# Masked maxima of the latent scores: a mask added and minimised by VectorE in place of mask products on TensorE, for query blocks 3, 2 and 0

## The chip, the cores and the metric

The kernel runs on one core of a Trainium2 chip. The metric is the device time of one execution in microseconds (us), the median of the runs that were taken. A core has five engines that work side by side, each through its own queue in order: TensorE (PE in the profile, with its weight loads as PEld), VectorE (DVE), ScalarE (ACT), GpSimd (POOL) and SyncE (SP, which here issues DMAs). Operands lie in SBUF, 128 partitions wide; TensorE writes its products to PSUM, which has eight banks of 128 x 512 f32.

## What is computed

The input is 8 sequences of 512 tokens with 128 channels. Three blocks follow each other:

```
x = x + 0.5 * ffn(layernorm(x))     # two layers of local attention and a gated feed-forward
x = x + attn(layernorm(x))          # "latent" attention, causal, 16 heads of 8 channels
x = x + 0.5 * ffn(layernorm(x))     # the same two layers again
```

The change lies in the middle block, whose core is

```
q_lat = einsum('bqhd,hdl->bhql', q, k_eff)
attn  = einsum('bhql,bkl->bhqk', q_lat, c_kv) / sqrt(hs)
attn  = softmax(where(causal, attn, -inf))
y_lat = einsum('bhqk,bkl->bhql', attn, c_kv)
```

The kernel folds the weight matrices beforehand, so that a head is a product of 8 channels of a projected q with 8 channels of a projected k.

## The kernel before

The program has three parts, in this order: the first feed-forward part `ffn("f0")`, `latent_attention()`, and the second feed-forward part `ffn("f1")`. The two `ffn` parts are written out by a planner (`Plan`) with step costs and due times; the diff leaves it alone. The latent part is written in program order, and TensorE keeps that order (`in_order`). The other engines follow from the data.

**Layout of the latent part.** Each of the 16 heads lies in a quarter of the partitions (`quadrant(g)`, 32 partitions, g from 0 to 3) and a place j from 0 to 3. A product of two 32-partition slices uses one quarter of the rows of TensorE's array, so products of different g can run beside each other. The queries of a sequence are cut into NB = 4 blocks of P = 128.

**Two passes over the scores.** The softmax needs a maximum per query before it takes exponentials. So the scores of a sequence are formed twice. The *maxima* pass forms them with queries on the partitions (tile `sc`), masks them causally and takes the maximum along the keys. The negative maxima are collected in the tile `lnm` (`maxima_of(b)[0]`), transposed by TensorE (tile `tp_nm`, L1524), copied to SBUF (L1530) and sent by a DMA (L1534) into a spare row of q. The *sums* pass forms the scores again with keys on the partitions (tile `st`), with the maximum already subtracted through that row. ScalarE takes their exponentials from PSUM (L1565, tile `pl`), and TensorE multiplies those with the values (L1571, tile `lo`).

**Ten pieces, four quadrants.** `SUMS` and `MAXIMA` each cut the work of one sequence into ten pieces that fill a PSUM bank of 512 columns. For the maxima they are: four pieces of query block 3 alone (512 keys), four of block 2 (384 keys) beside block 0 (128 keys), and two of block 1 for two heads (2 x 256 keys):

```
MAXIMA = (
    [[((3, j), 0)] for j in range(4)]
    + [[((2, j), 0), ((0, j), 3 * P)] for j in range(4)]
    + [[((1, j), 0), ((1, j + 1), 2 * P)] for j in (0, 2)]
)
```

The loop in `latent_attention` runs over the sequences b = 0 to 6. For each it goes through the ten pieces of the sums of sequence b and takes with each one piece of the maxima of sequence b + 1; each piece is done for the four quadrants. This text calls one quadrant of one such pair of pieces a *unit*: 7 x 10 x 4 = 280 units in the latent part. Sequence 0's maxima are done by the plan of `f0`, the sums of sequence 7 by the plan of `f1`.

**One unit.** `by_turns` deals the TensorE instructions of `sum_products` (bank `st`) and `maximum_products` (bank `sc`) alternately. Each list opens with four mask products in bf16 (L1545, L1487), which write the causal mask into the diagonal blocks of the bank, and then adds the products of q and k in f32 (L1554, L1496), one for each query block held. Each f32 product shows up as two records in the trace. Then ScalarE takes the exponentials of `st`, and `maximum` reduces `sc` on VectorE with one TENSOR_REDUCE of 512 columns: L1513 writes straight to `lnm`, L1509 (blocks 2 and 0) writes partial maxima of 128 columns to `lnb`. `maxima_end` (L1520, L1521) merges `lnb` into `lnm` once per sequence.

**PSUM.** The latent part has eight banks in one ring, `unit_bank`. A unit takes two, so TensorE can be at most four units ahead of the slower of ScalarE and VectorE.

**Between the units.** After five of the ten pieces, and again after the tenth, TensorE does other work of the sequence: transposes of earlier results (L1654), which VectorE divides by the sums (L1579, L1580) and GpSimd adds to X (L1586), products with the values (L1571), and projections of a later sequence (L1622, L1627, L1635). So each sequence has two stretches of 20 units, called stretch 1 (the four pieces of block 3 and the first of blocks 2 and 0) and stretch 2 (the other three of blocks 2 and 0 and the two of block 1), with TensorE's other work in the gaps between them. After stretch 2, TensorE transposes the maxima (L1524) before it goes on.

One operation elsewhere matters as a model: in the local attention of `ffn`, L777 is `nc.vector.tensor_tensor_reduce` on 128 x 128 scores in PSUM with a mask tile in SBUF; it adds, scales and keeps the minimum in an accumulator output.

Of the kernel before, what the change touches and what calls it, by code (L numbers as in the profile page):

```python
# [9 lines left out]
F32 = mybir.dt.float32  # L10
BF16 = mybir.dt.bfloat16
AF = mybir.ActivationFunctionType
ALU = mybir.AluOpType
# [3 lines left out]
P = 128  # L17
MASKED = -1.0e30
# [253 lines left out]
def kernel(  # L272
# [21 lines left out]
    nc = tc.nc  # L294
    B, T, C = x.shape
# [99 lines left out]
    def quadrant(g):  # L395
        return slice(32 * g, 32 * g + 32)
# [1199 lines left out]
    def latent_attention():  # L1596
        def in_order(ins):
            tc.keep_in_program_order(ins)

        count = [0]  # L1600

        def unit_bank(name):
            count[0] += 1
            return psum["s"].tile([P, 512], F32, tag="sc", name=f"{name}_{count[0]}")

        dealt = [0]

        def two_tiles():
            tag, *first, shape = PLACES[dealt[0] % len(PLACES)]
            dealt[0] += 1  # L1610
            if first:
                return [
                    flat(wk.tile(shape, F32, tag=f"{tag}{first[0] + n}", name=f"pl{dealt[0]}_{n}"))
                    for n in range(2)
                ]
            t = flat(wk.tile(shape, F32, tag=tag, name=f"pl{dealt[0]}"))
            return [t[:, :512], t[:, 512:]]

        def turn_into(xT, xn, b):
            tp = unit_bank(f"tp_lat_{b}")  # L1620
            for i in range(NB):
                in_order(nc.tensor.transpose(tp[:, i * P : (i + 1) * P], xn[:, i], ident))  # L1622
            nc.scalar.copy(xT, tp)

        def project(n, b, xT):
            ps = unit_bank(f"pq_{b}")
            in_order(nc.tensor.matmul(ps, lhsT=full[n], rhs=xT, start=True, stop=True))  # L1627
            fl = wk.tile([P, T], F32, tag=f"ge{n}", name=f"fl{n}_{b}")
            nc.scalar.copy(fl, ps)
            spread(heads("qk"[n], b), fl, "qk"[n])  # L1630

        def project_values(b, xT):
            ps = unit_bank(f"pv_{b}")
            for i in range(NB):
                in_order(nc.tensor.matmul(  # L1635
                    ps[:, i * C : (i + 1) * C], lhsT=xT[:, i * P : (i + 1) * P], rhs=full[2],
                    start=True, stop=True,
                ))
            value_copy(heads("v", b), ps)

        def multiply(b, j, todo):

            o = unit_bank(f"lo_{b}")
            for n, (c, at, tiles) in enumerate(todo):
                for ins in value_part(b, j, c, at, tiles, o, n == 0, n == NB - 1):
                    in_order(ins)
            os_ = wk.tile([P, INNER // P, P], F32, tag=f"oT{j % 2}", name=f"os_{b}_{j}")
            nc.scalar.copy(flat(os_), o)
            updates.append((b, j, flat(os_)))

        def update(b, j, os_):
            tp = unit_bank(f"tp_o_{b}")
            for i in range(NB):
                in_order(nc.tensor.transpose(  # L1654
                    tp[:, i * P : (i + 1) * P], os_[:, i * P : (i + 1) * P], ident
                ))
            rs = wk.tile([P, NB, 4], F32, tag=f"lrs{j % 2}", name=f"lrs_{b}_{j}")
            on = wk.tile([P, NB, 4, MD], F32, tag=f"lon{j % 2}", name=f"lon_{b}_{j}")
            quotients(tp, rs, on)
            add_tokens(b, j, on)  # L1660

        updates = left["updates"]
        ready = left["values"]
        turned, normed = {}, {}

        def norm(b):
            normed[b] = wk.tile([P, NB, C], F32, tag=f"hs{b % 2}", name=f"xn_{b}")
            ln_apply(normed[b], X[:, b], f"lat_{b}")

        norm(2)  # L1670
        ahead = [(b, held) for b in range(1, B) for held in MAXIMA]

        def heads_ahead(b):
            xT = turned[b] = wk.tile([P, T], F32, tag=f"fT{b % 2}", name=f"xT_{b}")
            turn_into(xT, normed.pop(b), b)
            return lambda: [project(n, b, xT) for n in range(2)]

        heads_ahead(2)()
        for b in range(B - 1):
            parts = {}  # L1680
            for s, held in enumerate(SUMS):
                other = ahead.pop(0) if ahead else None
                tiles = {}
                for half in (0, 1):
                    two = two_tiles()
                    for n in range(2):
                        g = 2 * half + n
                        bank = unit_bank(f"st_{b}")
                        units = [sum_products(b, held, g, lambda bank=bank: bank)]
                        if other is not None:  # L1690
                            mb, mheld = other
                            mbank = unit_bank(f"sc_{mb}")
                            units.append(
                                maximum_products(mb, mheld, (g + 2) % 4, lambda mbank=mbank: mbank)
                            )
                        by_turns([
                            [lambda ins=ins: in_order(ins()) for ins in unit] for unit in units
                        ])
                        sum_exponential(two[n], bank)
                        tiles[g] = two[n]  # L1700
                        if other is not None:
                            maximum(maxima_of(mb), mheld, (g + 2) % 4, mbank)
                for (c, j), at in held:
                    parts.setdefault(j, []).append((c, at, tiles))
                    if len(parts[j]) == NB:
                        ready.append((b, j, parts[j]))


                if s == len(SUMS) // 2 - 1:
                    while updates:  # L1710
                        update(*updates.pop(0))
                    project_ahead = heads_ahead(b + 2) if 0 < b < B - 2 else None
                    while ready:
                        multiply(*ready.pop(0))
                    if project_ahead is not None:
                        project_ahead()
            while updates:
                update(*updates.pop(0))
            if b > 0:
                project_values(b + 1, turned.pop(b + 1))  # L1720
            m = maxima_of(b + 1)
            maxima_end(m)
            tp = unit_bank(f"tp_nm_{b + 1}")
            in_order(maxima_turn(m, tp))
            shift_in(b + 1, shift_rows(b + 1, tp))
            while ready:
                multiply(*ready.pop(0))
            if b + 3 < B:
                norm(b + 3)
# [92 lines left out]
```

## Time and profile before

| what | value |
|---|---|
| median of 3 runs | 1708.36 us (1701.99 to 1709.99) |
| the profiled execution, whole | 1703.49 us |
| its span, first to last instruction | 1701.7 us |
| mean granted TensorE clock | 0.991 of full speed |
| busy over the span | PE 96%, DVE 79%, ACT 78%, POOL 68% |
| units of the latent part, first to last reduction | 726.7 to 989.4 us |
| VectorE reductions of the units: L1513 / L1509 | 168 / 112, mean 0.68 us each |
| mask products of the maxima (L1487) | 1120 in the units, four in each |

The span is the time from the first to the last instruction. The page gives busy shares over the whole span, and the stages of this kernel differ: GpSimd is nearly idle in the latent part and busy in the others. A duration is the time from the start to the end of one instruction; two instructions in a row on VectorE overlap a little, so the distance from start to start is shorter than the duration. The view by windows gives each engine's busy time in a stretch of the span, the timeline gives instructions in order of time with their start, and the view of waits gives who waited for whom.

### The profile page before, as it was taken

The page shows a single profiled execution, that of the slowest core. Times are in us where ns is not written, and L with a number is a line of the kernel's source. Part 1 is how long each engine was busy: PE and PEld are TensorE (multiplying, and loading weights), DVE is VectorE, ACT ScalarE, POOL GpSimd, SP SyncE. Part 2 cuts the span into 40 slices and gives each one's busy share as a digit, 9 for nine tenths or more (in the row PEclk, how much of TensorE's full clock was granted, in tenths as well). Part 3 has the DMA queues.
Part 4 walks back from the last instruction along what each step waited for, and adds up shares of the span by engine and source line. Part 5 has one row for each costly group of instructions (what it writes and reads, how often), then busy time and mean ns, then how long its engine had stood idle before and what let it go on. Part 6 is the DMA issues. An engine that isn't in the chain of part 4 may idle for free. (4 is left out here: it accounts for less than half of the span.)

```text
span 1701.7 us, 51528 instructions
## 1 busy us (share of the span) xinstructions
PE 1633.8 (96%) x19360; PEld 1146.6 (67%) x19360; DVE 1339.2 (79%) x4484; ACT 1329.3 (78%) x3913; POOL 1161.6 (68%) x1919
## 2 busy tenths in 40 slices
PE   5999999999999999999999999999999999999997
PEld 2666666676776676577777755766766666676675
DVE  6988888888888885867776655988888888888884
ACT  4888888888888885267766667988888888888883
POOL 8999998888788887000000056999887888878882
PEclk9999999999999999999999999999999999999998
DMA  5110111111111110000000001111111111111111
GB/s 168 29 36 20 27 26 27 33 27 28 35 27 26 27 30 9 16 17 17 17 16 17 16 9 29 33 27 26 27 26 27 27 32 30 28 31 26 27 30 41
DMA packets 51560, 49.48 MB, mean 29 GB/s; under 512 B 22726, under 2 KB 34544, under 8 KB 51312
## 3 DMA queue, kind: packets, MB, share of 16 engines
q1 hardware_dynamic: 51168, 45.41, 11.1%
q8 instruction: 153, 2.51, 0.6%
q14 instruction: 95, 0.78, 0.2%
q10 hardware_dynamic: 144, 0.79, 0.1%
HBM read 6.30 MB, written 2.10 MB: 5 GB/s over the span
## 5 line engine op out<-in xcount | busy, mean ns | idle before, releaser
L785 ACT ACTIVATE pr_f<-pr_f,nm_f 128x128 f32<-128x128 f32 x1024 | 397.4, 396 | 0.8 <-DVE nm_f L777 0.7
L634 PE MATMUL mm_f<-wqkv,hT_f 128*128 128x512 f32 x768 | 388.8, 600 | 1.7 <-DVE hT_f L612 1.4
L668 POOL TENSOR_TENSOR qk_f<-c_f,s_f 128x512 f32<-128x512 f32 x256 | 325.8, 1275 | 64.6 <-DVE s_f L647 30.7
L777 DVE CUSTOM_DVE_ANT_0 pr_f<-sc_f,band,q_f 128x128 f32<-128x128 f32 x1024 | 293.5, 345 | 46.9 <-PE sc_f L769 46.6
L792 POOL TENSOR_TENSOR pr_f<-pr_f,rso_f 128x512 f32<-128x512 f32 x256 | 264.9, 1042 | 12.6 <-DVE rso_f L811 7.9
L644 DVE TENSOR_TENSOR c_f<-mm_f,tab 128x512 f32<-128x512 f32 x256 | 174.2, 680 | 50.2 <-PE mm_f L634 31.5
L1586 POOL TENSOR_TENSOR X<-X,lon 128x128 f32<-128x128 f32 x26 | 11.3, 457 | 280.4 <-DVE lon L1580 280.4
L785 ACT ACTIVATION_READ_ACCUMULATOR pr_f<-pr_f,nm_f 128x1 f32 x1024 | 198.9, 194 | 0.0
L596 PEld LDWEIGHTS mm_f<-ident,qk_f 128*128 128x128 f32 x1024 | 121.3, 141 | 93.6 <-issue 63.4
L943 PE MATMUL mm_f<-fT_f,w 128*128 128x512 f32 (+1 forms) x384 | 182.2, 603 | 0.0
L647 DVE TENSOR_TENSOR s_f<-mm_f,tab 128x512 f32<-128x512 f32 x256 | 174.1, 680 | 0.0
L1565 ACT ACTIVATE pl<-st 128x512 f32<-128x512 f32 x280 | 156.0, 596 | 19.0 <-PE sc L1496 5.9
L660 ACT ACTIVATE sq_f<-mm_f 128x512 f32<-128x512 f32 x256 | 149.9, 595 | 21.5 <-PE mm_f L634 16.0
L852 PEld LDWEIGHTS mm_f<-pT_f,V_f 128*64 128x64 f32 x4096 | 130.2, 138 | 53.9 <-issue 23.9
L697 DVE TENSOR_REDUCE squares<-sq_f 128x16 f32<-128x1024 f32 x128 | 155.2, 1213 | 14.0 <-ACT sq_f L660 14.0
L596 PE MATMUL mm_f<-ident,qk_f 128*128 128x128 f32 x1024 | 156.3, 276 | 4.5 <-POOL qk_f L711 3.5
L596 PEld LDWEIGHTS mm_f<-ident,pr_f 128*128 128x128 f32 x1024 | 118.6, 141 | 55.9 <-POOL pr_f L792 26.5
L596 PE MATMUL mm_f<-ident,pr_f 128*128 128x128 f32 x1024 | 148.2, 275 | 6.5 <-POOL pr_f L792 6.0
L876 PEld LDWEIGHTS mm_f<-wo,oT_f 128*128 128x128 f32 x1024 | 129.7, 192 | 35.0 <-issue 18.9
L852 PE MATMUL mm_f<-pT_f,V_f 128*64 128x64 f32 x4096 | 147.7, 225 | 0.2 <-ACT pT_f L833 0.2
L634 PEld LDWEIGHTS mm_f<-wqkv,hT_f 128*128 128x128 f32 x768 | 122.0, 193 | 37.0 <-issue 24.3
L769 PE MATMUL sc_f<-kT_f,qT_f 64*64 64x128 f32 x4096 | 141.6, 276 | 0.0
(184 smaller groups left out, 3875.5 us busy)
## 6 DMA issues: line engine op xcount, KB each, us to landing
V_f<-V_f SPq DMA_DIRECT2D x224, 128.0 KB
hs_f<-Y SPq DMA_DIRECT2D x32, 112.0 KB
X<-in_x_dram SPq DMA_DIRECT2D x8, 256.0 KB
out_dram<-hs_f SPq DMA_DIRECT2D x6, 256.0 KB
Y<-fl SPq DMA_DIRECT2D x32, 32.0 KB
kT_f<-fl SPq DMA_DIRECT2D x32, 32.0 KB
V_f<-fl SPq DMA_DIRECT2D x32, 32.0 KB
wqkv<-in_wqkv_dram ACTq DMA_DIRECT2D x1, 768.0 KB
```

The costliest lines, as they stand in the source:

```text
L596: nc.tensor.transpose(dst[:, i * P : (i + 1) * P], src(i), ident)
L634: nc.tensor.matmul(ps.tile, lhsT=hT[:, i * P : (i + 1) * P], rhs=wqkv_sb[l][:, at * INNER : (at + 1) * INNER], start=True, stop=True,)
L644: nc.vector.tensor_mul(c1.tile, psv, tabs[l][:, 2 * s, i].unsqueeze(1).to_broadcast([P, H, DH]))
L647: nc.vector.tensor_mul(s1.tile.rearrange("p h (t d) -> p h t d", t=2), psv.rearrange("p h (t d) -> p h t d", t=2)[:, :, ::-1], tabs[l][:, ...
L668: lambda s=s, c1=c1, s1=s1: nc.gpsimd.tensor_add(qk[:, s].rearrange("p (h d) -> p h d", d=DH), c1.tile, s1.tile),
L697: nc.vector.tensor_reduce(z[:, 0], sq.tile.rearrange("p s (h d) -> p (s h) d", d=DH), AX.X, ALU.add)
L777: nc.vector.tensor_tensor_reduce(pr[:, h], sv[:, h % 2, h // 2], bands[1 if i else 0], scale=q8[:, h : h + 1], scalar=-MASKED, op0=ALU.add ...
L785: nc.scalar.activation(pr[:, h], pr[:, h], AF.Exp, bias=nm[:, h : h + 1], scale=-1.0, accum_out=sums[:, h : h + 1],)
L792: nc.gpsimd.tensor_mul(pr[:, heads], pr[:, heads], inv[:, heads].unsqueeze(2).to_broadcast([P, H // 2, P]),)
L852: nc.tensor.matmul(o[r * DH : (r + 1) * DH, u * P + w * WIN : u * P + (w + 1) * WIN], lhsT=(V2, V)[w][:, i, h * DH : (h + 1) * DH], rhs=pT ...
L943: nc.tensor.matmul(ps[: hsz[c], :], lhsT=w1_sb[l][:, at + c * P : at + c * P + hsz[c]], rhs=fT.tile, start=True, stop=True,)
L1565: nc.scalar.activation(dst, bank, AF.Exp, scale=MSCALE)
```

## The change

Eight of the ten pieces of the maxima, those of block 3 and those of blocks 2 and 0, lose their mask products on TensorE. Their products of q and k go unmasked into the bank (`plain_products`). On VectorE, `masked_maximum` does one `tensor_tensor_reduce` for each query block held: it adds a mask tile, changes the sign and keeps the minimum in the accumulator output, which goes straight to `lnm`. A piece of block 3 takes one such operation of 512 columns, a piece of blocks 2 and 0 takes two, of 384 and of 128 columns. The sums that it also writes go to a scratch tile, in two places by turns. The mask tile `past` holds zeros and, in its last 128 columns, the causal triangle; a block of n keys uses its last n columns. Mask and scratch lie in the room of the tile `u0` of the feed-forward part, and GpSimd fills the mask once. The pieces of block 1 stay as they were. `maxima_end` is no longer called for sequences 1 to 7; it stays for sequence 0.

In the changed program, each masked operation is two instructions on VectorE, the operation and the read-out of its accumulator. From the third masked operation on, each waits for TensorE's products and for the masked operation two before it, which wrote the same scratch place; the second operation of a piece waits for the latter only. The two GpSimd instructions that fill the mask stand between the last fill of a value tile (L1172) and the second fill of Y (L1195). TensorE, ScalarE and SyncE keep the order of what is left to them.

```diff
+        room = wk.tile([P, NHC, T], F32, tag="u0", name="room_lat")
+        past = room[:, 0]
+        nc.gpsimd.memset(past, 0.0)
+        nc.gpsimd.affine_select(
+            out=past[:, T - P :], in_=past[:, T - P :], pattern=[[-1, P]],
+            compare_op=ALU.is_ge, fill=MASKED, base=0, channel_multiplier=1,
+        )
+
+        def plain_products(b, held, g, bank):
+            rows = quadrant(g)
+            qp, kp = heads("q", b), heads("k", b)
+            return [
+                lambda i=i, j=j, at=at: nc.tensor.matmul(
+                    bank()[:, at : at + (i + 1) * P], lhsT=qp[rows, j, i * P : (i + 1) * P],
+                    rhs=kp[rows, j, : (i + 1) * P], start=True, stop=True, skip_group_check=True,
+                )
+                for (i, j), at in held
+            ]
+
+        thrown = [0]
+
+        def masked_maximum(m, held, g, bank):
+            for (i, j), at in held:
+                thrown[0] += 1
+                size = (i + 1) * P
+                nc.vector.tensor_tensor_reduce(
+                    room[:, 1 + thrown[0] % 2, :size], bank[:, at : at + size],
+                    past[:, T - size :], scale=-1.0, scalar=-MASKED,
+                    op0=ALU.add, op1=ALU.min, accum_out=m[0][:, g, j, i : i + 1],
+                )
...
                             mb, mheld = other
                             mbank = unit_bank(f"sc_{mb}")
+                            plain = mheld[0][0][0] > 1
                             units.append(
-                                maximum_products(mb, mheld, (g + 2) % 4, lambda mbank=mbank: mbank)
+                                (plain_products if plain else maximum_products)(
+                                    mb, mheld, (g + 2) % 4, lambda mbank=mbank: mbank
+                                )
                             )
...
                         if other is not None:
-                            maximum(maxima_of(mb), mheld, (g + 2) % 4, mbank)
+                            (masked_maximum if plain else maximum)(
+                                maxima_of(mb), mheld, (g + 2) % 4, mbank
+                            )
...
             m = maxima_of(b + 1)
-            maxima_end(m)
```

## The prediction, made before the changed kernel ran

> **What bounds the kernel now.** I read the page first, then the units through the windows, VectorE's timeline and the waits, and last TensorE between the stretches. The page's first part and its rows by slice (the latent part is slices 18 to 24, counted from 1):
>
> ```profile
> PE 1633.8 (96%) x19360; PEld 1146.6 (67%) x19360; DVE 1339.2 (79%) x4484; ACT 1329.3 (78%) x3913; POOL 1161.6 (68%) x1919
> ...
> PE   5999999999999999999999999999999999999997
> ...
> DVE  6988888888888885867776655988888888888884
> ```
>
> By these rows TensorE is the bound and VectorE has a quarter or more to spare in the latent part. That average hides two different stages. The windows show one sequence's stretch 1 and the gap behind it (busy us of each engine), and VectorE's timeline gives the same stretch:
>
> ```profile
> 762.09:774.06 11.97, 11.97 (x257) 10.45 (x247) 11.97 (x20) 10.91 (x20) 0.00 (x0) 1.00 0.01 3
> ...
> 774.15:780.94 6.79, 6.79 (x74) 2.88 (x73) 4.06 (x25) 2.64 (x6) 0.88 (x2) 1.00 0.01 4
> ```
>
> ```profile
> 762.09 9.66 DVE L1513 TENSOR_REDUCE lnm<-sc 128x1 f32<-128x512 f32 x16 [5.22 <-PE sc L1496]
> 771.67 2.48 DVE L1509 TENSOR_REDUCE lnb<-sc 128x4 f32<-128x512 f32 x4
> 774.06 0.45 DVE L1579 RECIPROCAL lrs<-tp_o 128x16 f32<-128x16 f32 x2
> ```
>
> VectorE is busy 11.97 of 11.97 us and does 20 reductions: one starts every 11.97 / 20 = 0.598 us, with no pause. The reader should see in the waits that this holds in all 14 stretches:
>
> ```profile
> DVE lnb L1509 <- PE sc L1496: 39.4, 7, 7.5
> DVE lnm L1513 <- PE sc L1496: 33.3, 7, 5.4
> ```
>
> The columns are the total wait in us, how often, and the longest. For 280 reductions there are just 14 waits for TensorE, one ahead of each stretch. So **within a stretch VectorE sets the pace**, and TensorE, which is bound to it by the ring of eight banks, is counted busy meanwhile because its products overlap and lie long. TensorE's own pace shows at the start of a stretch, where banks are still free: the first pair of units starts at 800.19 and the next at 801.26, which is 0.535 us a unit. In the gaps TensorE sets the pace, with one operation behind the other:
>
> ```profile
> 773.12 1.09 PE L1654 MATMUL tp_o<-ident,os 128*128 128x128 f32 x8
> 774.05 0.60 PE L1622 MATMUL tp_lat<-ident,xn 128*128 128x128 f32 x4
> 774.58 4.51 PE L1571 MATMUL lo<-pl,V_f 128*32 128x512 f32 x64
> ...
> 780.94 0.18 PE L1545 MATMUL st<-causal_t,rows_of 32*128 32x32 bf16 x1
> ```
>
> Note the overhang: TensorE begins its other work at 773.12, and VectorE ends its reductions at 774.06.
>
> **What a masked operation costs.** L777 is the same operation at 128 columns, also with scores in PSUM and a mask in SBUF:
>
> ```profile
> 301.94 0.35 DVE L777 CUSTOM_DVE_ANT_0 pr_f<-sc_f,band,q_f 128x128 f32<-128x128 f32 x1 [0.66 <-PE sc_f L769]
> 302.21 0.08 DVE L777 DVE_READ_ACCUMULATOR2_ANT nm_f<- 128x1 f32 x1
> ...
> 303.03 1.21 DVE L697 TENSOR_REDUCE squares<-sq_f 128x16 f32<-128x1024 f32 x1
> ```
>
> Four such operations with their read-outs lie between 301.94 and 303.03, which is 0.272 us each, start to start. The width is priced by additions of two operands, one of them in PSUM:
>
> ```profile
> L644 DVE TENSOR_TENSOR c_f<-mm_f,tab 128x512 f32<-128x512 f32 x256 | 174.2, 680 | 50.2 <-PE mm_f L634 31.5 <-POOL qk_f L668 8.2 <-ACT sq_f L660 5.3
> L1580 DVE TENSOR_TENSOR lon<-tp_o,lrs 128x128 f32<-128x128 f32 x26 | 6.1, 276 | 0.0
> ```
>
> 384 more columns take 0.680 - 0.276 = 0.404 us. So 512 columns take 0.272 + 0.404 = 0.676 us and 384 take 0.272 + 0.269 = 0.541 us. A unit of block 3 goes from 0.598 to 0.676 us (+0.078), a unit of blocks 2 and 0 from 0.598 to 0.541 + 0.272 = 0.813 us (+0.215). The ends: below, the operation at 512 columns can't be under the plain addition, which starts every 0.598 us, and a unit of blocks 2 and 0 not under 0.661 (two additions, 0.598 - 0.134 and 0.197, the step of L884 at 128 columns). Above, by the steepest row: L697 reduces 1024 columns in 1.247 us start to start, so 0.649 for 512 more, or 0.487 for 384; that makes 0.76 for 512 and 0.87 for the pair. I take 0.676 and 0.813, since L777 is the operation itself and only its width is carried over.
>
> A rule that speaks against this: the Trainium skill, "Vector Engine (DVE) Microarchitecture Reference", section "Points that are easy to get wrong", says that the form with two f32 sources in SBUF and an accumulator runs at half rate. Here one source is in PSUM, as in L777, where 128 columns at half rate would take 0.269 of its 0.272 us and leave nothing for the fixed cost; so the trace does not agree for this form, and the sum goes by its row. By the rule a column would take twice the 1.05 ns of the additions, an estimated 1.1 us for a unit's 512.
>
> **The other parts.**
> - *The wait for the masked operation two before* (scratch by turns): the pair L1579, L1580 has the same distance, and its first L1580 starts 0.174 us behind the second reciprocal, the usual step of that operation. I cost it at nothing. If it were exposed, L1520 shows a wait for the instruction just before: 0.12 us, which times 336 masked operations is 40 us more at the very most. Behind it on VectorE only the next maxima are queued.
> - *Mask products taken from TensorE*: 4 in each of 224 units, 896 in all. TensorE has 0.598 - 0.535 = 0.06 us a unit to spare already, so within a stretch they give nothing. At the start of a stretch the first `sc` is ready sooner: its f32 products begin 0.17 us after the first mask product (800.36 against 800.19). I take 0.15 us for each of the two stretches, with 0 and 0.5 as ends.
> - *`maxima_end`*: L1509 at 788.96, the next reduction at 789.88: 0.92 instead of 0.598. It saves 0.32 us a sequence, all of it on VectorE's path.
> - *Filling the mask on GpSimd*: it stands ahead of L1195, before which GpSimd waits 15.2 us for VectorE (697.45). The first unit starts at 726.7. Nothing, even if L1195 moves by its own 1.8 us.
> - *Plan parts*: no step moves, and `u0` is next written by `f1` long after the last unit. Nothing.
>
> **The sum.** Stretch 1: sixteen units of block 3 add 16 x 0.078 = 1.25 us. Its last four, of blocks 2 and 0, would add 4 x 0.215 = 0.86 us, but TensorE needs only the banks of the unit four back to finish its last unit. It leaves for the gap as soon as VectorE is done with unit 16, so these 0.86 us fall beside the gap's 7.8 us, where VectorE has 2.7 us to spare (4.06 of 6.79 busy). If that cover fails, 7 x 0.86 = 6 us more. Stretch 2: twelve units of blocks 2 and 0 add 12 x 0.215 = 2.58 us; the eight of block 1 that follow are unchanged, so TensorE leaves as late behind VectorE as before. Together 1.25 + 2.58 - 0.32 - 0.30 = **+3.2 us a sequence, +22.5 us for seven**. Against the profiled execution this is 1703.5 + 22.5 = 1726.0. The median of the runs lies 4.9 us above that execution, and by it the sum is 1730.9. I forecast 1728, between the two.
>
> **The rivals.**
> - *The extra time is hidden* (0.10): VectorE waits 72.7 us in all ahead of the stretches, and the operations add about 30. For: that idle time is there. Against: it lies where TensorE is late, and the ring lets VectorE trail by four units only. If stretch 2 hid its surplus like the end of stretch 1, about 1.2 us a sequence would stay: +8, 1714.
> - *TensorE was the pace, and it gets shorter* (0.05), faster: it decides if a masked unit takes no more than 0.598 us. Then the pace falls towards TensorE's 0.535: 32 masked units x 0.05, plus 0.6 at starts and `maxima_end`, 2.2 us a sequence: -15, 1690. For: PE 96%. Against: 20 reductions without a pause.
> - *Width costs more* (0.07): by the upper ends, 16 x 0.16 + 12 x 0.27 - 0.6 = 5.2 us a sequence: +36, 1742.
> - *TensorE's clock drops* (0.08): the granted clock is 0.83 in 660 to 680, where TensorE waits. Within a stretch TensorE then has 0.53 us of work in 0.68 or 0.81. At half clock it would need 1.07 a unit; for a quarter of the 224 units that is 56 x 0.33 = 18 us more, 1746. Against: units lie longer than their step, so some quarter of the array is always at work. The Trainium skill, "TensorE: Matmul & The Clock Gate", section "Why this matters for your kernels", warns of idle gaps over about 3 us; no gap here would come near that.
>
> **Chances.** Forecast 0.70; the rivals as given. About 0.5% (8.5 us) is what a measurement of this kernel can tell from no change: faster 0.05, within 0.10, slower 0.85. The range reaches from 1712 (the upper part of "hidden") to 1744 (wide operations, or all covers gone: 22.5 + 6 + 7 on the median). It leaves out the faster case and the upper half of the clock case.
>
> **What would show it.** Right: L1633 at 512 columns starts every 0.67 us, a pair of 384 and 128 every 0.81; VectorE without pause in the stretches; stretch 1 near 14.1 us (12.0 before) and stretch 2 near 14.5 (12.4 before); still 14 waits for `sc`; the gaps from VectorE's end to its next start shorter by 0.9 us after stretch 1 and unchanged after stretch 2; one sequence 42.6 us long instead of 39.4. Wrong: waits for `sc` inside a stretch (TensorE or its clock), starts 0.1 us later than 0.676 (the wait of distance two), or a half clock within 725 to 1015.

## The result, and the profile after

| what | before | after |
|---|---|---|
| median of 20 runs each | 1708.01 us | 1716.64 us |
| ratio | | 1.0054 [1.0039 to 1.0069] |
| the profiled execution, whole | 1703.49 us | 1719.03 us |
| its span | 1701.7 us | 1717.2 us |
| mean granted TensorE clock in it | 0.991 | 0.984 |
| the units, TensorE's first to last product | 263.1 us | 269.0 us |
| one sequence, from stretch 1 to the next stretch 1 | 39.41 us | 40.10 us |

The changed kernel is slower, as forecast, but by 8.6 us where some 20 were expected. The difference of the two profiled executions, 15.5 us, is larger, and only 5.9 us of it lie in the units. The page of the changed kernel, its row of busy times, VectorE's row by slice and the granted clock by slice:

```profile
PE 1650.3 (96%) x18464; PEld 1155.5 (67%) x18464; DVE 1351.2 (79%) x4918; ACT 1334.4 (78%) x3913; POOL 1161.4 (68%) x1921
...
DVE  6888888888888885877766744988888888888884
...
PEclk9999999999999999999999979999999999999998
```

TensorE has 896 instructions less, and its busy time is 16.5 us more: it is counted busy while it is bound to another engine, or runs at half clock. The single 7 in the row of the clock is slice 24, just behind the units. The windows of VectorE's stretch 1, of the gap behind it and of stretch 2 show the same picture as before (after the length: busy us of PE, PEld, DVE, ACT, POOL, then the granted clock):

```profile
763.26:775.93 12.67, 12.67 (x194) 10.61 (x188) 12.67 (x49) 11.06 (x20) 0.00 (x0) 1.00 0.01 3
775.93:783.39 7.46, 7.46 (x97) 3.70 (x99) 4.05 (x26) 3.23 (x7) 0.95 (x2) 1.00 0.01 3
783.39:796.76 13.37, 13.37 (x247) 12.82 (x243) 13.37 (x57) 11.66 (x20) 0.00 (x0) 1.00 0.14 42
```

The same view of before for VectorE's stretch 2 (that of stretch 1 stands in the prediction):

```profile
782.37:794.66 12.29, 12.29 (x286) 11.84 (x279) 12.25 (x22) 11.01 (x20) 0.00 (x0) 1.00 0.14 44
```

VectorE works without a pause through both stretches, at full TensorE clock, as forecast. But stretch 1 lasts 12.67 us and not 14.1, and stretch 2 13.37 and not 14.5. The reason stands in VectorE's timeline of that stretch:

```profile
763.26 0.69 DVE L1633 CUSTOM_DVE_ANT_0 room_lat<-sc,room_lat 128x512 f32<-128x512 f32 x1 [5.07 <-PE st L1545]
763.87 0.08 DVE L1633 DVE_READ_ACCUMULATOR2_ANT lnm<- 128x1 f32 x1
763.87 0.69 DVE L1633 CUSTOM_DVE_ANT_0 room_lat<-sc,room_lat 128x512 f32<-128x512 f32 x1
...
773.04 0.55 DVE L1633 CUSTOM_DVE_ANT_0 room_lat<-sc,room_lat 128x384 f32<-128x384 f32 x1
...
773.52 0.29 DVE L1633 CUSTOM_DVE_ANT_0 room_lat<-sc,room_lat 128x128 f32<-128x128 f32 x1
...
773.75 0.56 DVE L1633 CUSTOM_DVE_ANT_0 room_lat<-sc,room_lat 128x384 f32<-128x384 f32 x1
```

An operation of 512 columns starts 0.611 us after the one before it (0.676 forecast). A pair of 384 and 128 columns takes 0.709 us (0.813 forecast). The row of 128 columns has its next start after 0.21 to 0.23 us (0.211 where an unmasked operation follows, 0.227 where a masked one does), and L777 at the same width after 0.272. The rows also name what differs: L777 reads `sc_f,band,q_f`, this operation `sc,room_lat`. The third name is L777's scale, one value per partition in a tile; `masked_maximum` has the constant -1.0.

The waits for TensorE are 15 where 14 were forecast:

```profile
DVE room_lat L1633 <- PE sc L1620: 32.4, 7, 6.3
DVE room_lat L1633 <- PE st L1545: 31.1, 6, 5.2
...
DVE room_lat L1633 <- PE st L1554: 2.2, 2, 1.9
```

Fourteen stand ahead of a stretch. The fifteenth, 0.28 us at 869.64, is inside the second stretch of the fourth sequence and lengthens it by 0.36 us; it comes back at the same place in e1, e5, e6 and e12, and its cause is open.

### The profile page after: what moved, and what is told of

It is laid out like the page before. It is cut to its first block, busy times and chain, and to the rows that moved or that the text cites. A ratio compares the mean times of both kernels' runs of the same rounds, so it can differ in the third digit from the quotient of the medians.

```text
span 1717.2 us, 50381 instructions
## 1 busy us (share of the span) xinstructions
PE 1650.3 (96%) x18464; PEld 1155.5 (67%) x18464; DVE 1351.2 (79%) x4918; ACT 1334.4 (78%) x3913; POOL 1161.4 (68%) x1921
## 5 line engine op out<-in xcount | busy, mean ns | idle before, releaser
L634 PE MATMUL mm_f<-wqkv,hT_f 128*128 128x512 f32 x768 | 393.3, 607 | 1.6 <-DVE hT_f L612 1.4
L777 DVE CUSTOM_DVE_ANT_0 pr_f<-sc_f,band,q_f 128x128 f32<-128x128 f32 x1024 | 293.2, 344 | 47.7 <-PE sc_f L769 47.3
L1633 DVE CUSTOM_DVE_ANT_0 room_lat<-sc,room_lat 128x384 f32<-128x384 f32 (+1 forms) x336 | 148.8, 510 | 65.7 <-PE sc L1620 32.4
L1565 ACT ACTIVATE pl<-st 128x512 f32<-128x512 f32 x280 | 160.8, 598 | 20.5 <-PE st L1554 11.8
```

Of the source, the lines that this page charges most:

```text
L634: nc.tensor.matmul(ps.tile, lhsT=hT[:, i * P : (i + 1) * P], rhs=wqkv_sb[l][:, at * INNER : (at + 1) * INNER], start=True, stop=True,)
L777: nc.vector.tensor_tensor_reduce(pr[:, h], sv[:, h % 2, h // 2], bands[1 if i else 0], scale=q8[:, h : h + 1], scalar=-MASKED, op0=ALU.add ...
L1565: nc.scalar.activation(dst, bank, AF.Exp, scale=MSCALE)
```

## The experiments

The first theory, **A**: an operation with a constant scale is cheaper by a fixed amount than one whose scale lies in a tile, and everything else went as forecast. Its rival, B: the operation is cheaper here for its place or tiles, not for its scale. The second theory, **C**: VectorE sets the pace of the units before and after, and the mask products taken from TensorE give only an earlier start of each stretch. Its rival: TensorE's relief hides a part of the added time. Each expectation spells out what it sets against these.

In the table, *units* is the time from TensorE's first to last product of the 280 units in the profiled run (263.1 us before, 269.0 after); the medians of before are from the same chip. The ratio is that of all runs on record, with its 95% interval, and not that of the two medians.

| run | median | before there | ratio | units |
|---|---|---|---|---|
| e1_ptr_scale | 1726.61 | 1704.00 | 1.0130 [1.0101 to 1.0159] | 283.7 |
| e2_l777_constant | 1700.81, one run | 1704.00 | | not changed |
| e3_only_block_3 | 1707.10 | 1704.00 | 1.0010 [0.9998 to 1.0023] | 263.6 |
| e4_only_blocks_2_0 | 1708.73 | 1704.00 | 1.0022 [1.0010 to 1.0035] | 267.9 |
| e5_changed_again | 1708.29 | 1708.15 | 1.0017 [1.0001 to 1.0033] | 269.1 |
| e6_mask_twice | 1711.27 | 1708.15 | 1.0020 [1.0011 to 1.0029] | 272.6 |
| e7_no_mask_products | 1704.53 | 1708.15 | 0.9982 [0.9973 to 0.9991] | 260.1 |
| e8_two_aside | 1705.10 | 1708.15 | 0.9982 [0.9973 to 0.9991] | 266.1 |
| e9_two_aside_late | 1707.17 | 1704.08 | 1.0011 [1.0000 to 1.0022] | 262.7 |
| e10_near_scratch | 1759.23, one run | 1704.08 | | 319.1 |
| e11_one_aside_late | 1704.22 | 1704.08 | 1.0004 [0.9994 to 1.0015] | 263.2 |
| e12_seam_filled | 1717.80 | 1704.08 | 1.0072 [1.0059 to 1.0086] | 269.0 |

The runs are compared by their units below, since the time of a whole run also depends on where TensorE's clock drops outside the units (last part of this section).

**e1: the scale in a tile.** The changed kernel with one edit:

```diff
+        minus = const.tile([P, 1], F32, name="minus")
+        nc.gpsimd.memset(minus, -1.0)
...
-                    past[:, T - size :], scale=-1.0, scalar=-MASKED,
+                    past[:, T - size :], scale=minus[:, 0:1], scalar=-MASKED,
```

> The changed kernel, but the scale of the masked operation comes from a 128x1 tile that holds -1.0 instead of the constant -1.0, as L777 takes its scale from q8. Theory A (the size of the masked operation was carried over from L777, whose scale operand in a tile costs about 0.06 us an instruction): masked operations of 512 columns start every 0.67 us instead of 0.611, a pair of 384 and 128 every 0.82 instead of 0.709; stretch 1 takes 16 x 0.06 = 1.0 us longer from TensorE's first to TensorE's last product, stretch 2 takes 12 x 0.12 = 1.4 us longer; +16 us over the changed kernel, about 1733 us. Rival B (L777 is slow for where it stands, beside a busy GpSimd, or for its mask and output tiles): 0.611 and 0.709 as in the changed kernel, and about 1717 us.

VectorE's timeline of this run:

```profile
768.03 0.75 DVE L1635 CUSTOM_DVE_ANT_0 room_lat<-sc,room_lat,minus 128x512 f32<-128x512 f32 x1
...
768.70 0.75 DVE L1635 CUSTOM_DVE_ANT_0 room_lat<-sc,room_lat,minus 128x512 f32<-128x512 f32 x1
...
779.45 0.35 DVE L1635 CUSTOM_DVE_ANT_0 room_lat<-sc,room_lat,minus 128x128 f32<-128x128 f32 x1
...
779.72 0.62 DVE L1635 CUSTOM_DVE_ANT_0 room_lat<-sc,room_lat,minus 128x384 f32<-128x384 f32 x1
```

The steps are 0.671 us at 512 columns and 0.538 + 0.271 = 0.809 for a pair: the forecast's 0.676 and 0.813 almost to the digit. Stretch 1 lasts 14.06 us, stretch 2 14.59, a sequence 42.29 (forecast 14.1, 14.5, 42.6). The units are 20.6 us longer than before, the median 22.6 us. So the forecast is the right one for a kernel that keeps the scale in a tile, and the tile makes an operation 0.055 to 0.060 us longer at all three widths, and a pair 0.100 us. It also shows who sets the pace: TensorE's stretch 1 grows from 12.38 to 13.34 us and its stretch 2 from 13.58 to 14.79, which are the 16 x 0.060 and 12 x 0.100 us added on VectorE, with nothing hidden.

**e2: the model operation with a constant.** The kernel before, with the scale of L777 changed in the same way but in the other direction; this leaves out the division by the norm of q in the local attention:

```diff
-                        scale=q8[:, h : h + 1], scalar=-MASKED, op0=ALU.add, op1=ALU.min,
+                        scale=-8.0, scalar=-MASKED, op0=ALU.add, op1=ALU.min,
```

> The kernel before, with the scale of L777 as the constant -8.0 instead of the tile q8; this leaves the division by the norm of q out of the local attention, so its output is not the reference's. Theory A: L777 starts every 0.211 us instead of 0.271. Rival B: it stays at 0.271, since its place and tiles are the same. Whether the time moves is open; VectorE is not the bound there by the page (79%), so between 1690 and 1709 us.

Its timeline, at the place that the prediction showed of before:

```profile
301.70 0.29 DVE L777 CUSTOM_DVE_ANT_0 pr_f<-sc_f,band 128x128 f32<-128x128 f32 x1 [0.66 <-PE sc_f L769]
301.91 0.08 DVE L777 DVE_READ_ACCUMULATOR2_ANT nm_f<- 128x1 f32 x1
...
302.55 1.22 DVE L697 TENSOR_REDUCE squares<-sq_f 128x16 f32<-128x1024 f32 x1
```

Four operations from 301.70 to 302.55 are 0.212 us each, where they were 0.272: the same 0.060 us, in another part of the kernel and with other tiles. B falls. The local attention has 1024 of these operations, 61 us of VectorE; the one run is 3 us below the median of before, so that VectorE time is mostly not on the path there.

**e3 and e4: one part of the change alone.** The condition `mheld[0][0][0] > 1` becomes `== 3` (block 3 alone, with `maxima_end` kept) and `== 2` (blocks 2 and 0 alone).

> Only the four pieces of block 3 are masked on VectorE; blocks 2 and 0 keep their mask products, L1509 and maxima_end. By the trace after: sixteen operations of 0.611 against 0.598 add 0.2 us to stretch 1, an earlier first sc takes 0.15 back; stretch 2 stays. Theory C (all that the change costs comes from the pieces of blocks 2 and 0): within 1 us of the kernel before, 1707 to 1709 as a median. Rival D (something outside the units costs some 3 us as soon as the mask tile is there): +3 us.

> Only the four pieces of blocks 2 and 0 are masked on VectorE; block 3 keeps its mask products and L1513. By the trace after: the four units at the end of stretch 1 hide behind TensorE's other work, so stretch 1 stays within 0.1 us from TensorE's first to its last product; stretch 2 takes 0.7 us longer (12 x 0.11, less 0.3 for maxima_end and 0.3 for the earlier first sc). Theory C: 7 x 0.7 = +5 us. Rival D: +8 us, as the whole change.

The units grow by 0.6 us (e3) and by 4.9 us (e4), together 5.4 of the 5.9 us. So the edit of block 3 costs almost nothing, since 0.611 against 0.598 us is paid back by the earlier first bank of stretch 1. The pair of two operations in place of one reduction is what costs.

The medians say less. That of e3 lies 3.1 us above before, and not within the expected 1 us; 3 us is what rival D forecasts. Six of its ten runs have a mean clock of 0.988, for four of the nineteen of before. At 0.991 the averages are 1705.4 and 1703.8 us, and of the 2.1 us between the profiled spans 1.7 lie ahead of the units, which begin at 727.1 us and not at 725.4. That start varies from 724.9 us (e5) to 727.8 (e1) over the runs, apart from e2, whose edit lies ahead of it; e5 has the mask tile too, so the tile is not the cause.

**e5: the changed kernel again**, on another chip.

> The changed kernel once more, beside the others. Its units take 5.9 us more than before in the first profile (269.0 against 263.1 us from TensorE's first to its last product), and the whole run 8.6 us more. Theory E (what is left is the half clock at the seams, whose length differs from run to run): at equal mean clock it is 6 to 7 us above the kernel before. Rival D (a fixed cost outside the units): 8 to 9 us above at equal clock, and a place in the trace where it arises every time.

The units are 6.0 us longer, as in the first profile, but the median is the same as that of before on this chip. The clocks are not the same: eight of the eleven runs have 0.992, and 29 of the 33 of before have 0.988, so the comparison at equal clock that theory E asks for can't be made here. On the two other chips five runs of before have 0.992 and average 1703.1 and 1703.4 us; the eight here average 1708.1, some 5 us more. D, a fixed cost outside the units, is not seen: in the profile of e5 the units begin 0.5 us earlier than before, and what follows them is 1.0 us shorter.

**e6 and e7: the mask products.** e6 is the changed kernel with the mask products of `maximum_products` kept, so that TensorE has all its former work:

```diff
-                                (plain_products if plain else maximum_products)(
+                                maximum_products(
```

> VectorE's part alone: the masked operations as in the change, but TensorE keeps its mask products too, so the mask is added twice. Theory C (the mask products are worth only the earlier first sc of each stretch): VectorE's steps stay 0.611 and 0.709, the first reduction comes 1.31 and 1.43 us after TensorE's first product instead of 1.16, and the units take (0.15 + 0.27) x 7 = 2.9 us more than the changed kernel. Rival F (TensorE is the pace): pauses for sc inside the stretches, 10 us or more.

e7 is the kernel before, with the products of these eight pieces unmasked and still reduced by L1513 and L1509. The causal mask is left out of the maxima of query blocks 3, 2 and 0, and the exponent is scaled by 1/100:

```diff
-                                maximum_products(mb, mheld, (g + 2) % 4, lambda mbank=mbank: mbank)
+                                (plain_products if plain else maximum_products)(
...
-    MSCALE = float(MD) ** -0.5
+    MSCALE = 0.01 * float(MD) ** -0.5
```

> TensorE's part alone: no mask products for blocks 3, 2 and 0, but L1513, L1509 and maxima_end as before. The maxima run over future keys too, and the scale of the exponentials is a hundredth of the kernel's, so the output is not the reference's. Theory C: reductions every 0.598 us, units 2.9 us shorter than before, about 0.2% faster. Rival F (TensorE is the pace): the steps fall towards 0.53 us and the time by some 15 us.

Stretch 1 and stretch 2 of VectorE in e6, and the same two in e7:

```profile
763.89:776.56 12.67, 12.67 (x260) 10.90 (x249) 12.67 (x49) 11.07 (x20) 0.00 (x0) 1.00 0.02 4
784.38:797.75 13.37, 13.37 (x286) 12.65 (x279) 13.37 (x57) 11.56 (x20) 0.00 (x0) 1.00 0.14 40
```

```profile
761.59:773.56 11.97, 11.97 (x187) 10.21 (x178) 11.97 (x21) 10.93 (x20) 0.00 (x0) 1.00 0.01 2
781.51:793.80 12.29, 12.29 (x247) 11.82 (x243) 12.25 (x23) 11.45 (x20) 0.00 (x0) 1.00 0.15 45
```

With the mask products back (e6), the masked operations keep their 0.611 us and no wait appears inside a stretch beyond the one told above; the first reduction of a stretch is late by 1.31 and 1.43 us as before the change, and not by 1.16 and 1.17. The units are 3.6 us longer than in the changed kernel, 7 x (0.15 + 0.26) = 2.9 of it by these starts. Without the mask products and without masked operations (e7), the reductions keep their step of 0.598 us, and the units are 3.0 us shorter; the first stretch, part of it at half clock, takes back 0.55 us of what the others gain. In both runs a sequence changes by 0.52 us, 0.41 of it at the starts; the other 0.1 was not traced. So 896 products on TensorE are worth 3.6 us, most of it at the start of a stretch, and VectorE's stretches have the same length with and without them. C stands. TensorE is not the pace, in spite of its 96%.

**e8, e9, e11: work taken from VectorE.** If VectorE sets the pace, what it does less should shorten the stretch. In e8 ScalarE copies the bank of two units of stretch 1 to SBUF, and VectorE is to reduce the copies later; the program order left that to the data:

```diff
+        def aside(m, held, g, bank):
+            part = room[:, len(later)]
+            nc.scalar.copy(part, bank)
+            later.append((m, held, g, part))
...
-                            maximum(maxima_of(mb), mheld, (g + 2) % 4, mbank)
+                            (aside if g == 3 and s in (1, 3) else maximum)(
+                                maxima_of(mb), mheld, (g + 2) % 4, mbank
+                            )
...
+                    while later:
+                        maximum(*later.pop(0))
```

> From the kernel before: in stretch 1, ScalarE copies the banks of two of the twenty units to SBUF, and VectorE reduces them in the gap that follows, where it has time. Theory C (VectorE is the pace in the stretches): stretch 1 takes 18 x 0.598 us instead of 20 x 0.598, 1.0 to 1.2 us less, so 7 to 8 us in all, about 0.4% faster than before. Rival G (ScalarE, with 22 operations, becomes the pace): 0.3 us less or nothing. Rival H (VectorE's additional work in the gap delays the next stretch): slower.

It did not do what was meant: VectorE took each copy up right behind ScalarE (copy at 767.66, reduction at 768.27, in the middle of the stretch) and waited 0.23 and 0.63 us for the two. The units are 3 us longer, and nothing follows for the pace; that its median is below that of before goes with the clock of its runs, 0.992 against mostly 0.988, and not with its units. In e9 the reductions of the copies are held at the end of the stretch, by keeping VectorE's maxima in program order. e11 does the same with one unit (`s == 3`).

> The kernel before, with two of the twenty units of stretch 1 (the fourth quadrant of the second and of the fourth piece) copied by ScalarE to SBUF and reduced by VectorE only at the end of the stretch, where TensorE has gone on to its other work. The computation is whole. If VectorE alone sets the pace of a stretch and its work behind unit 16 is covered by the gap, stretch 1 ends 2 x 0.598 = 1.2 us earlier for TensorE (12.41 to 11.2 us), a sequence takes 38.2 us instead of 39.4, and the units 263.1 - 8.4 = 254.7 us. Rival: ScalarE, busy 10.91 of 11.97 us in the stretch, gets two copies of 0.47 us more and becomes the pace at 11.85 us; then stretch 1 is shorter by 0.1 us at most and the units take 262 to 263 us.

> As the run with two units set aside, with one (the fourth quadrant of the fourth piece). If VectorE alone sets the pace: stretch 1 shorter by 0.598 us, units of 263.1 - 4.2 = 258.9 us. If ScalarE is the pace as soon as it has to copy: units of 262 to 263 us. If one copy fits beside the exponentials (10.91 + 0.47 = 11.38 us) and two don't, this run gains about as much as the run with two or more.

The units take 262.7 and 263.2 us for 263.1 before: next to nothing is gained, as the rivals say. That ScalarE is the pace does not follow. The window of VectorE's stretch 1 in e9:

```profile
761.48:773.22 11.74, 11.74 (x255) 10.65 (x245) 11.25 (x19) 11.37 (x22) 0.00 (x0) 1.00 0.01 3
```

VectorE is busy 11.25 of 11.74 us and now waits; ScalarE has 11.37, two copies more than its 10.9 of before. But its operations overlap a little, and where nothing holds them they start every 0.48 to 0.49 us (in e9 at 765.84, 766.32, 766.80 and 767.28), so 22 of them would need less than 11 us by an estimate from these steps. The timelines of e11 show what holds the stretch:

```profile
771.62 0.58 ACT L1613 COPY room_lat<-sc 128x512 f32<-128x512 f32 x1
771.89 1.29 DVE L1509 TENSOR_REDUCE lnb<-sc 128x4 f32<-128x512 f32 x2 [0.27 <-PE sc L1496]
```

The copy stands behind the exponentials of the same unit and frees the bank of unit 16 at 772.20, which is 10.96 us after TensorE's first product of the stretch (761.24); before, VectorE's reduction of unit 16 ends 10.97 us after it (in e9 the second copy ends after 10.90). TensorE's last unit needs this bank, four units back, and so begins no earlier. VectorE, one reduction ahead, waits for the next product, whose bank it had itself freed no earlier than before. So the runs show that a reduction moved here is not time won; they do not show ScalarE as the pace. A unit costs 0.598 us of VectorE, 0.535 of TensorE and 0.48 to 0.49 of ScalarE, and none of these versions has units shorter by more than 0.4 us.

**e10: the wait that was costed at nothing.** All masked operations write one scratch place, so that each waits for the one just before it:

```diff
-                    room[:, 1 + thrown[0] % 2, :size], bank[:, at : at + size],
+                    room[:, 1, :size], bank[:, at : at + size],
```

> The changed kernel, with every masked operation writing the same scratch place, so that each waits for the masked operation right before it and not for the one two before. If that wait costs what L1520 shows (0.12 us) and the distance of two is what hides it, the operation of 512 columns starts every 0.73 us instead of 0.611 and the pair every 0.95 instead of 0.709: 16 x 0.12 + 12 x 0.24 = 4.8 us a sequence, units of 269.0 + 33 = 302 us. If the read-out of the accumulator between the two operations covers the wait anyway, the steps stay at 0.611 and 0.709 and the units at 269 us.

VectorE's timeline:

```profile
793.98 0.56 DVE L1633 CUSTOM_DVE_ANT_0 room_lat<-sc,room_lat 128x384 f32<-128x384 f32 x1 [1.80 <-PE sc L1620]
...
794.58 0.29 DVE L1633 CUSTOM_DVE_ANT_0 room_lat<-sc,room_lat 128x128 f32<-128x128 f32 x1
...
795.03 0.56 DVE L1633 CUSTOM_DVE_ANT_0 room_lat<-sc,room_lat 128x384 f32<-128x384 f32 x1
```

From 384 to 128 columns it is 0.601 us instead of 0.483 (+0.118, the price that L1520 shows), from 128 to the next 384 it is 0.443 instead of 0.227 (+0.216), and from 512 to 512 it is 0.844 instead of 0.611 (+0.233). The last two also wait for TensorE's products, which by the timeline are there before; that this second wait is what doubles the price fits the rows but was not tested apart from the widths. The units grow by 50 us over the changed kernel. The two places by turns are therefore worth 50 us, and the wait at distance two costs at most the 0.016 us by which 0.227 exceeds 0.211.

**e12: the seam, and where the rest of the time is.** The profiled executions differ by 15.5 us, of which 9.6 come behind the units. TensorE's clock tells where. Two windows of the changed kernel's first profile, and the same two of e5, the same program (columns as above; the clock is the third number from the right):

```profile
1003.00:1006.40 3.40, 2.10 (x20) 1.19 (x19) 2.50 (x13) 2.64 (x7) 1.53 (x9) 1.00 0.00 0
...
1006.40:1033.70 27.30, 27.28 (x142) 12.06 (x141) 7.76 (x20) 9.83 (x19) 19.43 (x33) 0.50 0.05 11
```

```profile
1002.50:1005.90 3.40, 2.18 (x20) 1.26 (x20) 2.46 (x12) 2.67 (x7) 1.46 (x8) 1.00 0.00 0
...
1005.90:1033.20 27.30, 25.56 (x208) 11.99 (x209) 14.74 (x39) 16.27 (x34) 26.12 (x47) 1.00 0.09 20
```

At the seam between the latent part and `f1`, TensorE waits for ScalarE, 0.76 and 1.17 us at a time. In the first execution its clock is half for the next 27.3 us, in which it does 142 products instead of 208; in the second it stays full. The profile of before has a half clock of 3.4 us there. Other profiles have 0 (e4, e6, e8, e10), 3.4 (e1, e3, e9, e11), 6.8 (e2) and 13.7 us (e7). For the changed kernel on its first chip, eleven runs with a mean clock of 0.986 lie at 1716.9 us on average and the two at 0.992 at 1709.2; before, on the chip of e9, has fifteen runs at 0.991 (1704.3) and three at 0.988 (1709.5).

The long half clock is not spread evenly over the kernels. A mean clock of 0.986 or less (the profile with the 27.3 us has 0.984) stands in 17 of the 31 runs of the changed kernel (14 of 20 on the first chip, 3 of 11 in e5) and in four of the six of e12. None of the 75 runs of before on the three later chips has it, and none of the 80 of the other edits. So it goes with this program (e12 adds three products to it), though the place lies behind the changed part. The masked operations alone do not bring it: e1, e6 and e10 have them too, and in their 15 runs it is absent. What does is open.

The account closes for e5, whose other stretches of half clock are as long as those of before to within 3.4 us: units +6.0, half clock at the seam 3.4 us shorter, which saves up to 1.7, together +4.3; the span is 1706.2 - 1701.7 = 4.5 us longer. In the first profile 23.9 us more of half clock make up to 12 us, and 9.6 are seen. For the medians on the first chip, 8.6 us apart, it is argued and not shown that the 2.7 us beyond the units are half clock: the clocks of the twenty runs of before there are not on record.

e12 fills the first of TensorE's waits at the seam with products that nobody reads:

```diff
+        warm = unit_bank("warm")
+        for i in range(3):
+            in_order(nc.tensor.matmul(warm, lhsT=ident, rhs=past, start=True, stop=True))
```

> The changed kernel, with three products of 128x128 with 128x512 in f32, whose results nobody reads, behind the last products of the latent part, where TensorE waits 0.76 us for ScalarE. They take about 3 us of TensorE. If the half clock at the seam between the latent part and the second feed-forward part comes of TensorE's waits there, and if it is what spreads the changed kernel's times over 1708 to 1720 us, then it is gone in all or nearly all runs: mean clocks of 0.991 or more, and times that lie together at 1708 + 0 to 2 us. If these waits are not its cause, mean clocks of 0.984 to 0.986 stay in a part of the runs, with times of 1716 to 1722 us.

Windows of its seam:

```profile
1008.00:1011.40 3.40, 2.23 (x25) 1.14 (x20) 2.21 (x12) 1.85 (x7) 2.76 (x11) 1.00 0.00 0
1011.40:1014.80 3.40, 3.40 (x20) 1.11 (x20) 1.42 (x8) 1.14 (x2) 3.23 (x7) 0.50 0.00 0
```

The products lie at 1002.46 to 1005.3, and the window with the wait of 1.17 us, with TensorE busy 2.23 of 3.40 us, is followed by a half clock again, here of 3.4 us. Of six runs, four have a mean clock of 0.986 and 1718.4 us. So filling this wait does not remove it. That the later one, inside `f1`, is the cause is not shown: all profiles have it, 1.17 us long, and some have no half clock. Nor does the busy share of the 3.4 us ahead of the half clock decide: 0.62 (after), 0.66 (before, e12), 0.69 (e2) and 0.74 (e7) were followed by it, 0.64 (e5), 0.65 (e8) and 0.70 (e4) were not. Why it lasts 0, 3.4, 6.8, 13.7 or 27.3 us stays open.

## Why the prediction was right in its direction and too large

**The step that failed** is the price of the masked operation: "I take 0.676 and 0.813, since L777 is the operation itself and only its width is carried over." Not only its width differed. L777's scale is an operand in a tile and that of the changed kernel is a constant, and this is 0.060 us of each instruction: 0.611 measured for 0.676, and 0.709 for 0.813, where a pair is 0.100 us shorter by it. e1 and e2 show it from both sides. The width was carried over well: (0.611 - 0.211) / 384 is 1.04 ns a column, the additions gave 1.05. The lower ends named there, 0.598 and 0.661, lay nearer than the values chosen.

With the measured prices, stretch 1 grows by 16 x 0.013 = 0.2 us and loses 0.15 at its start, and stretch 2 grows by 12 x 0.111 = 1.33 and loses 0.32 and 0.26: about +0.8 us a sequence instead of +3.2. The profile has 40.10 - 39.41 = 0.69. Seven sequences are 4.8 us; the wait inside one stretch adds 0.36 and a slow first stretch 0.62, where the half clock ends at 726.5 us and not at 725.1, inside its first unit. Together 5.8 of the measured 5.9 us.

That the median of 1716.64 us lies between the forecast's 1712 and 1744 is luck: it does so by the half clock at the seam, which the sum does not contain. The two runs at a clock of 0.992 on the same chip average 1709.2 us, and the median of e5 is 1708.29. Nor does the rival "hidden", with its +8 us, fit by more than its number: VectorE's stretch 2 shows its whole surplus.

The other steps:

- *VectorE sets the pace within a stretch*: right (windows, e6, e7). The page's 96% for TensorE misleads, as the prediction said; e1 adds that what VectorE's operations gain in length the stretches gain too.
- *Mask products give nothing but the start*: right. The starts are worth 0.15 and 0.26 us, for 0.15 each, and another 0.1 us a sequence comes from elsewhere (e6, e7).
- *The last four units of stretch 1 are hidden*: right. VectorE ends 1.46 us behind TensorE's last product of the stretch, for 0.96 before, and TensorE's gap of 7.75 us is unchanged. VectorE's own gap shrinks from 8.23 to 7.46 us, for 0.9 forecast. e1 shows the cover holding for the larger surplus too.
- *`maxima_end` saves 0.32*: right. Stretch 2 of VectorE grows from 12.37 to 13.37 us, and 1.33 - 0.32 is 1.01.
- *The wait at distance two costs nothing*: right, at most 0.016 us. The bound of 40 us for the opposite was too low: e10 has 50, since two of its three kinds of step pay 0.22 to 0.23 us and not 0.12.
- *The fill of the mask is hidden*: right. The first product of the units starts at 725.36 us, before at 725.39.
- *The clock does not drop in the stretches*: right, 1.00 in the windows shown, but for the first unit. A half clock within 725 to 1015, named as a sign of being wrong, is there all the same: up to 726.5 us, and from 1006.4; before has one from 1001.6 to 1005.0. The rival looked for it in the stretches alone. The prediction had the row of half clock behind a TensorE wait (0.83 in 660 to 680) and did not ask about the seam with `f1`, which lies outside the changed part and moves the time by up to 10 us from one run to the next.

Half-rate operation, weighed in the prediction, is not seen: 512 columns take 0.611 us start to start.

The Trainium skill, "VectorE: DVE Perf Modes", section "Scalar operands", says that a scalar operand is a constant or one value per partition, and gives no price for either; the runs here give 0.060 us between them. On the clock, the skill, "TensorE: Matmul & The Clock Gate", section "Why this matters for your kernels", asks for idle gaps of no more than about 3 us. The waits at the seam are 1.17 us at most and the half clock came, so here the measurement decides against it; the same page, section "What's actually happening", has a free-running window of 3413 ns, and the lengths seen at the seam (3.4, 6.8, 13.7 and 27.3 us) are one, two, four and eight of these.

## What to carry to other kernels

A model row must agree with the new instruction in every operand, not only in its operation and its tiles: read the names on the right of the arrow and ask for each where it lies. Price the pace engine's step first, then the steps of the others. Before work is moved off the pace engine, ask when the engine that takes it will free the buffer: in e9 and e11 the copy freed it no earlier than the reduction had. And when two runs differ by more than the stage that was changed, look for half clock in the stages behind it, and count in how many runs of each kernel it stands.

## What the runs showed of the hardware

- A scale in a tile instead of a constant makes this operation of VectorE 0.060 us longer at 128 and 512 columns and 0.055 at 384 (e1, e2).
- With a constant scale the operation and its read-out take 0.078 us + 1.04 ns a column from start to next start: 0.211, 0.483 and 0.611 us at 128, 384 and 512.
- A wait of one VectorE operation for the one right before it costs 0.12 us; where the operation also waits for a product that is there already, 0.22 to 0.23 was seen, though the widths differ too; for the one two before, no more than 0.016 (e10).
- In nine of the fourteen profiles a half clock of TensorE begins at the seam behind 3.4 us in which it was busy for 0.62 to 0.74, with no wait over 1.2 us; in five it does not, among them e5, e8 and e4 with 0.64, 0.65 and 0.70. Of the two profiles of the changed kernel, one has 27.3 us of it and the other none.
